# Layer 0's third projection of two batches beside the first chain of squarings; the first score projection starts with products of h alone; other fillers at the entry

## The chip, the cores and the metric

The kernel runs on one core of one Trainium2 chip. The metric is device time in microseconds of one launch. All matrix work is in float32 on the matrix engine (PE), where one product of a 128x128 stationary block with 512 columns takes two passes. The other engines are the vector engine (DVE), the scalar engine (ACT), GpSimd (POOL) and SyncE (SP, which issues DMAs).

## The reference

Four layers are applied to x of shape (8, 512, 32, 32); a batch is a matrix of 512 channels by 1024 positions. Cut to what matters here:

```python
# layer 0: three 1x1 convolutions to 64 channels, two of them with batch norm over all batches
f_x = relu(batchnorm(conv1x1(x, Wf, bf))).reshape(b, 64, hw)
g_x = relu(batchnorm(conv1x1(x, Wg, bg))).reshape(b, 64, hw)
h_x = conv1x1(x, Wh, bh).reshape(b, 64, hw)
z = einsum('bcn,bcm->bnm', f_x, g_x)
sigma = svd(z)[:, 0]                       # the largest singular value
x = conv1x1(einsum('bnm,bcm->bcn', z / sigma, h_x), Wv, bv) + x
# layer 1: group norm, attention over 1024 positions with 512 channels, projection, + x
# layer 2: attention with 128 channels, projection, batch norm by given constants, + x
# layer 3: signs of x times signs of W, batch norm, + x, a shifted leaky relu
```

## The kernel before

**Layer 0 without its big matrix.** z is never formed. With F, G and H the 64 x 1024 matrices of a batch, F Fᵀ, G Gᵀ and H Gᵀ are 64 x 64 (function `gram`, L1445 to L1463). The largest singular value comes from repeated squarings of the small matrix (F Fᵀ)(G Gᵀ). Two batches share the 128 partitions, so there are four pairs and four chains of squarings. `order` takes batches 6 and 7 first, then 0 to 5: the pair of batches 6 and 7 (named `jl`) has the chain `first_chain` (L1129 on), which must end before the first batch can go on. The other pairs (`rest`) have the chain `chain` (L1025 on); its steps are drawn one by one from the generator `behind`, wherever the main program calls `next(behind)` or `chore`.

**The loop over batches** (L1342 on). x of each batch is loaded and multiplied with the weights of f, g and h (L1354; 16 pieces for f and g, 8 for h, each writing half of the partitions). f and g are copied out and their statistics gathered (`bn_stats`). The product of h gets its bias on ACT as `hraw`, and in the next batch `turn` (L1248 to L1254) transposes it on PE in four blocks and copies it to `ht_pair`. x of the last two batches stays in SBUF (`resident`).

**Weights.** Layer 1's four weight matrices are merged into two: `wu` from q and k, `wo` from v and p. `natural` (L1320 to L1325) transposes q, k and v through two PSUM tiles of two banks each, every group of eight transposes copied out by ACT and DVE, half each. `product` (L1394 to L1407) makes a merged matrix in 16 products. After the loop the batch norm's mean, variance and scale are formed (L1490 to L1511), and `relu` (L1481) applies it on ACT to f and g of a batch.

**Fillers.** The chain of squarings is serial: two small products (L1141, L1142), copied out by DVE and ACT, which the next two need. So the generator `filler` holds PE work that is put between its steps: transposes of v, the products of `wu`, the Gram product of h and g of the pair `jl`, the scaling of a later weight, the transposes and Gram products of the other three pairs with the bias sums (`biases`) between, and the products of `wo`. This stretch is under a manual schedule for PE: the program's order is PE's order. DVE's and ACT's order is set by a scheduler when the program is built[...].

**Entry of the first batch** (`entering(0)`, `enter`). `weights0` (L299) makes two small weights from the chain's result, then four visits correct x: two products (L420), an addition on DVE (L429) and statistics (L432). Two small products with a group matrix (L441 mean, L448 variance) follow, then the scale and bias of the group norm. Between these steps PE gets a number of fillers given by the tuple `(2, 1, 1, 1, 2, 2, 4)`; what is left follows.

**First u.** `normal` (L471) forms the normalised h (not to be confused with layer 0's) in eight tiles on DVE; `split_h` makes the sums T1 to T4 (L336 to L339). `make_u` forms the score projection u in two groups of seven products each (Winograd's form of a 2 x 2 block product; `seven`, L342 to L380). Products named A11·B11 and A12·B21 read h alone, the other five need sums of h. In `make_u` for the first batch a step of the chains is drawn after its steps 1, 4, 7, 10 and 13; in the scores of the first batch after the steps 1, 5, 9, 17 and 24 (L923).

Of the kernel before, what the change touches and what calls it, by code (L numbers as in the profile page):

```python
# [8 lines left out]
F32 = mybir.dt.float32  # L9
F16 = mybir.dt.float16  # L10
I32 = mybir.dt.int32
AF = mybir.ActivationFunctionType
# [4 lines left out]
P = 128  # L17
B = 8
C = 512
N = 1024  # L20
CC = C // P
NT = N // P
HF = 512
NH = N // HF
# [61 lines left out]
def kernel(  # L86
# [17 lines left out]
    nc = tc.nc  # L104
    mm = nc.tensor.matmul
# [17 lines left out]
    def bank():  # L123
        return psum["bank"].tile([P, HF], F32, tag="bank", name="bank")
# [17 lines left out]
    def half(i):  # L142
        return bass.ts(i, HF)

    def side(i):

        return slice(i * MID, (i + 1) * MID)
# [11 lines left out]
    early = ctx.enter_context(ExitStack())  # L159
# [179 lines left out]
        tt(t4, b21, t2, ALU.subtract)  # L339
        return {"B11": b11, "B21": b21, "B22": b22, "T1": t1, "T2": t2, "T3": t3, "T4": t4}  # L340

    def seven(term, c11, c12, c21, c22, b1=None, b2=None, exp=None, then=None):  # L342

        def move(dst, ps, bias):
            if bias is None:
                nc.scalar.copy(dst, ps)  # L348
            else:
                nc.scalar.activation(dst, ps, AF.Identity, bias=bias)  # L350

        def plus(ps, bias, u, dst):
            if bias is None:
                nc.vector.tensor_tensor(dst, ps, u, ALU.add)  # L354
            else:
                nc.vector.scalar_tensor_tensor(dst, ps, bias, u, ALU.add, ALU.add)

        pa, va = term(None, "A11", "B11", True, False)
        move(c11, va, None)
        yield  # L360
        pc, vc = term(None, "S1", "T1", True, False)
        move(c22, vc, None)
        yield
        term(pa, "S2", "T2", False, False)
        move(c12, va, None)
        yield
        term(pc, "S4", "B22", False, True)
        plus(vc, b1, c12, c12)
        yield
        term(pa, "S3", "T3", False, False)  # L370
        plus(va, b2, c22, c22)
        yield
        _, vb = term(None, "A12", "B21", True, True)
        plus(vb, b1, c11, c11)
        yield
        term(pa, "A22", "T4", False, True)
        if exp is None:
            move(c21, va, b2)
        else:
            nc.scalar.activation(c21, va, AF.Exp, scale=exp)  # L380
        if then is not None:
            then()
        yield
# [94 lines left out]
        b = [ht[:, chunks[k], half(n)] for k in range(2) for n in range(2)]  # L478
        return differences_of(b, [hs[:, i] for i in range(3)])

    def make_u(env, hb, got):

        ut = env["big"].tile([P, CC, N], F32, tag="uv", name="ut")
        wa = weights["u"]

        def done():
            us = env["big"].tile([P, 3, 2, HF], F32, tag="us", name="us")
            got.append(
                sums_of(quarters_of(ut, chunks, [half(0), half(1)]), [us[:, i] for i in range(3)])
            )  # L490

        for i in range(2):
            term = product_of(
                lambda a, b, q, k: wa[a][:, k, bass.ts(i, P)],
                lambda a, b, q, k: hb[b][:, k, :],
            )
            yield from seven(
                term,
                ut[:, i, half(0)],
                ut[:, i, half(1)],  # L500
                ut[:, 2 + i, half(0)],
                ut[:, 2 + i, half(1)],
                bu[:, i : i + 1],
                bu[:, 2 + i : 3 + i],
                then=done if i else None,
            )

    def make_v(hb, vt):

# [383 lines left out]
    def fast(env, n, hb, ua):  # L893


        b = order[n]
# [4 lines left out]
        def chore(now):  # L901
            if now:
                next(behind, None)

        es = [None] * NT
        for k, _ in enumerate(scores1(env, hb, ua, es)):
            if rest3 and k % 2 == 0:
                if next(rest3[0], "end") == "end":
                    rest3.pop()
                    if more and order[n + 1] not in resident:  # L910
                        resident[order[n + 1]] = load_x(order[n + 1])
            if n == 0 and k == 2:
                weights["o"] = sums_of(quarters_of(wo, chunks, cols2), [so[:, i] for i in range(3)], True)
            if n == 0 and k == 6:
                tp = quarters_of(sbw["tpg"], chunks, [slice(0, P), slice(P, 2 * P)])
                weights["tp"] = sums_of(tp, [sp[:, i] for i in range(3)], True)
            if k == 8 and more:
                ahead = entering(n + 1)


            if k in (10, 13, 20, 27):
                next(ahead, None)
            chore(n == 0 and k in (1, 5, 9, 17, 24))  # L923
        esum = es.pop()
        vt = env["big"].tile([P, NT, C], F32, tag="uv", name="vt")
        for k, _ in enumerate(make_v(hb, vt)):
# [415 lines left out]
    for b in range(B):  # L1342
        xt = load_x(b) if b else first
        for name, src, pool in later.get(b, ()):
            load_w(name, src, shapes.get(name, [P, CC, C]), pool)
        if b == 4:
            load_rows()
        if b >= B - 2:
            resident[b] = xt
        banks = [bank() for _ in w0]  # L1350

        def products(i, cc):
            for h in range(NH):
                mm(  # L1354
                    out=banks[i][side(h), :],
                    lhsT=w0[i][:, cc, :],
                    rhs=xt[:, cc, half(h)],
                    start=cc == 0,
                    stop=cc == CC - 1,
                )  # L1360

        if b == 0:
            for cc in range(CC):
                for i in range(2):
                    products(i, cc)
        for i in range(3):
            if b == B - 1 and i == 2:
                for _ in natural("q", "w3"):
                    pass
            if b or i == 2:  # L1370
                for cc in range(CC):
                    products(i, cc)
            if i == 0:
                nc.scalar.copy(fs[b], banks[i])
                nc.vector.bn_stats(st[:, 0, b, :], fs[b])
            elif i == 1:
                nc.vector.tensor_copy(gs[b], banks[i])
                nc.vector.bn_stats(st[:, 1, b, :], gs[b])
                if last is not None:
                    turn(last[0], last[1], ht_pair[last[0] // 2], 0)  # L1380
        hraw = a2.tile([P, HF], F32, tag="hraw", name="hraw")
        nc.scalar.activation(hraw, banks[2], AF.Identity, bias=bhc)
        last = b, hraw
        if b == 3:
            total3 = sign_weights()
        if b == 5:
            scale_signs(total3)
# [102 lines left out]
        nc.vector.bn_aggr(mv[:, i, :], st[:, i, :, :])  # L1490
    nat_k = natural("k", "q")
    next(nat_k)
    turn(last[0], last[1], ht_pair[last[0] // 2], 0)
    ps = bank()
    mm(out=ps[:, 0:2], lhsT=fold, rhs=mv[:, :, 0], start=True, stop=True)
    nc.vector.tensor_copy(mean, ps[:, 0:2])
# [36 lines left out]

    cols2 = [slice(0, C // 2), slice(C // 2, C)]

    def filler():

        yield from natural("v", "k")  # L1540
        load_w("p", w_p, [P, CC, C], a1, tag="v")
        yield from product(nat["q"], nat["k"], wu, True)
        yield from gram(jl, 2, ht_pair[jl], gtl)
        scale_z()
        yield
        between = biases()
        sums = sums_u()
        for j in rest:
            for _ in grams(j):
                next(sums, None)  # L1550
                yield
                if next(between, None):
                    yield
        yield from product(nat["v"], sbw["p"], wo, False)
# [11 lines left out]
    with tc.manual_schedule(engines={mybir.EngineType.PE}):  # L1566
        steps = entering(0)
        for k, _ in enumerate(first_chain(jl)):

            for _ in range(4 if k == 3 * NSTEP + 3 else 2 if k % 3 == 1 or k == 0 else 1):  # L1570
                next(todo, None)
            for args in (next(relus, None),):
                if args:
                    relu(*args)
        for n in (2, 1, 1, 1, 2, 2, 4):
            next(steps)
            for _ in range(n):
                next(todo, None)
        for _ in todo:
            pass  # L1580
# [9 lines left out]
    with ExitStack() as main:  # L1590
        psum_pools(main, 0, 8)
        big = main.enter_context(tc.tile_pool(name="big", bufs=1, reuse_waits="tile"))
        epool = main.enter_context(tc.tile_pool(name="epool", bufs=EBUFS))
        small = main.enter_context(tc.tile_pool(name="small", bufs=3))
        env.update({"big": big, "e": epool, "small": small})
        got = []
        hb = split_h(env, normal(env, resident[order[0]], True))

        for k, _ in enumerate(make_u(env, hb, got)):
            if k in (1, 4, 7, 10, 13):  # L1600
                next(behind)
        ua = got[0]
        for n in range(B):
            hb, ua = fast(env, n, hb, ua)
# [171 lines left out]
```

## Time and profile before

| | us |
|---|---|
| median of 3 runs | 1883.69 |
| lowest to highest | 1883.57 to 1885.51 |
| profiled execution, time | 1883.24 |
| profiled execution, span first to last instruction | 1881.5 |

The profiled execution as time stretches (us from the span's start), with the lines of the code:

| stretch | what runs |
|---|---|
| 4.9 to 97.3 | loop over batches; q is transposed from 91.9 |
| 97.3 to 102.9 | last transposes of h, transposes of k and v, scale of the batch norm |
| 102.9 to 112.9 | first products of wu, relu on ACT, Gram products of the pair jl |
| 112.9 to 157.3 | first chain of squarings and its fillers |
| 157.3 to 182.7 | weights of the entry, corrections, group norm, products of wo |
| 182.7 to 210.9 | h and first u |
| 210.9 to 265.8 | scores of the first batch |

From there every batch takes the same steps. The granted PE clock is 1.00 from 8 us on, but for one stretch in the entry (a window of 170 to 180 us shows 0.83) and the end. In a line of the timeline the first figure is the start, the second the duration, then engine, line, operation, what is written from what, shape and count; a bracket gives the idle time before on that engine and who ended it. PE counts are passes.

### The profile page before, as it was taken

To read this page: it belongs to the slowest core of one execution; us is meant where nothing else is said; L and a number is where in the kernel's file an instruction comes from. 1 tells how busy PE (TensorE), PEld (TensorE's weight loads), DVE (VectorE), ACT (ScalarE), POOL (GpSimd) and SP (SyncE) were. 2 spreads that over 40 slices of the span, in tenths; PEclk is the share of its full clock that TensorE was granted. 3 is DMA by queue.
4 is the path that set the end of the run, shared out by engine and by line. 5 is a ranking of instruction groups with operands and counts; after the bars stand their busy time and mean duration, and the time that the engine had idled before them with its cause. 6 is when DMAs were issued, how large, how long until landed. Compare 5 with 4: busy or idle time off the path is not lost.

```text
span 1881.5 us, 16558 instructions
## 1 busy us (share of the span) xinstructions
PE 1857.0 (99%) x6244; PEld 952.1 (51%) x6244; DVE 1118.1 (59%) x2077; ACT 545.7 (29%) x888; POOL 121.8 (6%) x109
## 2 busy tenths in 40 slices
PE   8998999999999999999999999999999999999997
PEld 3365455544645455544645455544645464544653
DVE  3256776467764676567764676357643666355447
ACT  2142221144202521244202522144202521244113
POOL 1000001100020000100020001100020001000011
PEclk9999999999999999999999999999999999999999
DMA  8420000002000200002000200001000200000001
GB/s 324 161 79 7 1 18 1 1 34 73 12 1 12 84 23 1 1 34 73 12 1 11 78 30 0 1 34 67 12 0 12 90 12 0 1 34 23 12 0 47
DMA packets 25203, 66.51 MB, mean 35 GB/s; under 512 B 3553, under 2 KB 4765, under 8 KB 24477
## 3 DMA queue, kind: packets, MB, share of 16 engines
q1 hardware_dynamic: 24188, 64.96, 9.5%
q8 instruction: 51, 0.84, 0.2%
q10 hardware_dynamic: 864, 0.43, 0.1%
q14 instruction: 36, 0.29, 0.0%
q0 software_dynamic: 64, 0.00, 0.0%
HBM read 46.44 MB, written 18.94 MB: 35 GB/s over the span
## 4 chain that ended last, share of the span: by engine, by line
PE 96%; DVE 2%; ACT 1%; issue 0%; DMA 0%; POOL 0%; DVEq 0%; ACTq 0%
PE bank L396 46%; PE bank L565 21%; PE bank L967 6%; PE bank L814 6%; PE bank L1354 5%; PE bank L666 3%; PE bank L683 3%; PE bank L420 1%; PE bank L706 1%; PE wide L1394 1%; PE bank L1450 1%; PE bank L1035 1%; PE bank L837 0%; PE quad L1248 0%; PE bank L1141 0%
## 5 line engine op out<-in xcount | busy, mean ns | idle before, releaser
L565 PE MATMUL bank<-e,vt 128*128 128x512 f32 x768 | 336.2, 594 | 0.0
L565 PEld LDWEIGHTS bank<-e,vt 128*128 128x128 f32 x768 | 144.3, 190 | 172.3 <-issue 167.9
L396 PE MATMUL bank<-ut,h 128*128 128x512 f32 x384 | 178.3, 597 | 0.0
L396 PEld LDWEIGHTS bank<-ut,h 128*128 128x128 f32 x384 | 71.3, 190 | 95.2 <-issue 93.5
L814 PE MATMUL bank<-tpg 128*128 128x512 f32 x256 | 115.4, 595 | 0.0
L396 PE MATMUL bank<-us,hs 128*128 128x512 f32 x256 | 115.3, 592 | 0.0
L967 PE MATMUL bank<-e,tpg 128*128 128x512 f32 x256 | 114.7, 595 | 0.0
L354 DVE TENSOR_TENSOR e<-bank,e 128x512 f32<-128x512 f32 x96 | 66.1, 689 | 63.2 <-PE bank L396 44.7
L821 ACT ACTIVATE e<-bank 128x512 f32<-128x512 f32 x128 | 76.3, 597 | 67.0 <-PE bank L814 67.0
L396 PE MATMUL bank<-wo,h 128*128 128x256 f32 x384 | 89.9, 384 | 0.0
L348 ACT COPY e<-bank 128x512 f32<-128x512 f32 x96 | 56.1, 584 | 115.0 <-PE bank L396 114.6
L396 PE MATMUL bank<-h,wu 128*128 128x512 f32 x192 | 89.4, 595 | 0.0
L236 POOL TENSOR_TENSOR r_r<-r_v,minus_half 128x4 f32<-128x4 f32 (+1 forms) x11 | 10.9, 988 | 1073.4 <-DVE r_v L235 1067.9
L967 PEld LDWEIGHTS bank<-e,tpg 128*128 128x128 f32 x256 | 48.1, 190 | 60.4 <-issue 60.0
L396 PEld LDWEIGHTS bank<-us,hs 128*128 128x128 f32 x256 | 48.6, 190 | 58.4 <-issue 55.7
L396 PEld LDWEIGHTS bank<-wo,h 128*128 128x128 f32 x384 | 71.4, 190 | 12.6 <-issue 3.8
L826 DVE TENSOR_TENSOR esum<-esum,e 128x1024 f32<-128x1024 f32 x48 | 58.8, 1225 | 30.2 <-ACT e L821 30.0
L814 PEld LDWEIGHTS bank<-tpg 128*128 128x128 f32 x256 | 47.6, 190 | 55.0 <-issue 52.4
L694 ACT ACTIVATE sg<-xt,rb 128x512 f16<-128x512 f32 x64 | 44.2, 716 | 107.4 <-DVE xt L685 104.5
L354 DVE TENSOR_TENSOR vt<-bank,vt 128x512 f32<-128x512 f32 x48 | 33.2, 691 | 67.3 <-PE bank L396 66.6
L348 ACT COPY vt<-bank 128x512 f32<-128x512 f32 x64 | 37.3, 583 | 122.3 <-PE bank L396 122.3
L348 ACT COPY ut<-bank 128x512 f32<-128x512 f32 x48 | 28.1, 585 | 123.4 <-PE bank L396 123.4
(367 smaller groups left out, 2927.0 us busy)
## 6 DMA issues: line engine op xcount, KB each, us to landing
xt<-in_x SPq DMA_DIRECT2D x55, 512.0 KB
out<-both SPq DMA_DIRECT2D x63, 256.0 KB
rfull<-r_dram SPq DMA_DIRECT2D x15, 512.0 KB
f_dram<-f SPq DMA_DIRECT2D x8, 256.0 KB
fb<-f_dram SPq DMA_DIRECT2D x8, 256.0 KB
w<-in_w SPq DMA_DIRECT2D x1, 1024.0 KB
q<-in_w_q SPq DMA_DIRECT2D x1, 1024.0 KB
k<-in_w_k SPq DMA_DIRECT2D x1, 1024.0 KB
```

Of the source, the lines that this page charges most:

```text
L348: nc.scalar.copy(dst, ps)
L354: nc.vector.tensor_tensor(dst, ps, u, ALU.add)
L396: mm(out=ps[:, q * w : (q + 1) * w], lhsT=lt(ka, kb, q, k), rhs=rhs(ka, kb, q, k), start=first and q == 0 and k == 0, stop=last and k == 1 ...
L565: mm(out=ps, lhsT=a[:, t, bass.ts(r_, P)], rhs=e[t], start=first and t == 0, stop=last and t == NTH - 1, skip_group_check=True,)
L666: mm(out=ps[:, i, :], lhsT=xt[:, cc, bass.ts(4 * h + i, P)], rhs=sbw["tpg"][:, cc, 2 * P : 3 * P], start=cc == 0, stop=cc == CC - 1,)
L683: mm(out=ps, lhsT=sbw["z"][:, bass.ts(oc, P)], rhs=att, start=True, stop=True)
L694: nc.scalar.activation(sg[:, cc, :], xt[:, cc, half(h)], AF.Sign, bias=rb3[:, cc : cc + 1])
L814: mm(out=ps, lhsT=pt[:, 0, bass.ts(t, P)], rhs=tt[:, 0, half(h)], start=True, stop=True,)
L821: nc.scalar.activation(e[:, half(h)], ps, AF.Exp, scale=float(P) ** -0.5)
L826: nc.vector.tensor_tensor(esum, esum, e, ALU.add)
L967: mm(out=banks[h], lhsT=gt[:, t, :], rhs=es[t][:, half(h)], start=t == 0, stop=t == NT - 1,)
L1354: mm(out=banks[i][side(h), :], lhsT=w0[i][:, cc, :], rhs=xt[:, cc, half(h)], start=cc == 0, stop=cc == CC - 1,)
```

## The change

The products of h for batches 6 and 7 leave the loop; a generator `late_h` makes them as fillers, one quarter at a time, between the products of `wu` and the Gram product that needs them. The loop takes two banks instead of three for these batches, and the transposes of `hraw` for batches 5, 6 and 7 move accordingly (that of batch 5 stays in the loop, those of 6 and 7 go into `late_h`). `seven` can draw its sixth step (A12·B21) ahead to second place, and `make_u` with `early` takes the first two steps of both groups first, then the rest of each. The first u draws no chain steps any more; the scores of the first batch draw ten instead of five. The entry's tuple of fillers gets larger.

```diff
-    def seven(term, c11, c12, c21, c22, b1=None, b2=None, exp=None, then=None):
+    def seven(
+        term, c11, c12, c21, c22, b1=None, b2=None, exp=None, then=None, early=False
+    ):
...
+        def second():
+            _, vb = term(None, "A12", "B21", True, True)
+            plus(vb, b1, c11, c11)
+
         pa, va = term(None, "A11", "B11", True, False)
         move(c11, va, None)
         yield
+        if early:
+            second()
+            yield
...
-        _, vb = term(None, "A12", "B21", True, True)
-        plus(vb, b1, c11, c11)
-        yield
+        if not early:
+            second()
+            yield
...
-        for i in range(2):
+        def group(i):
...
+        groups = [group(i) for i in range(2)]
+        for _ in range(2 * early):
+            for g in groups:
+                next(g)
+                yield
+        for g in groups:
+            yield from g
...
-            chore(n == 0 and k in (1, 5, 9, 17, 24))
+            chore(n == 0 and k in (1, 4, 7, 9, 11, 15, 17, 19, 23, 25))
...
-        banks = [bank() for _ in w0]
+        banks = [bank() for _ in w0[: 3 if b < B - 2 else 2]]
...
-            if b == B - 1 and i == 2:
-                for _ in natural("q", "w3"):
-                    pass
+            if i == 2 and b >= B - 2:
+                if b == B - 1:
+                    for _ in natural("q", "w3"):
+                        pass
+                continue
...
-    turn(last[0], last[1], ht_pair[last[0] // 2], 0)
...
+    def late_h(b):
+
+        ps = bank()
+        for cc in range(CC):
+            for h in range(NH):
+                mm(
+                    out=ps[side(h), :],
+                    lhsT=w0[2][:, cc, :],
+                    rhs=resident[b][:, cc, half(h)],
+                    start=cc == 0,
+                    stop=cc == CC - 1,
+                )
+            if cc < CC - 1:
+                yield
+        hraw = a2.tile([P, HF], F32, tag="hraw", name="hraw")
+        nc.scalar.activation(hraw, ps, AF.Identity, bias=bhc)
+        yield
+        turn(b, hraw, ht_pair[b // 2], 0)
...
         yield from product(nat["q"], nat["k"], wu, True)
+        for b in order[:2]:
+            yield from late_h(b)
         yield from gram(jl, 2, ht_pair[jl], gtl)
...
-        for n in (2, 1, 1, 1, 2, 2, 4):
+        for n in (2, 2, 2, 2, 4, 3, 6):
...
-        for k, _ in enumerate(make_u(env, hb, got)):
-            if k in (1, 4, 7, 10, 13):
-                next(behind)
+        for _ in make_u(env, hb, got, True):
+            pass
```

More of the change, by code (lines that the diff above doesn't have):

```diff
@@ L479, in split_h, with make_u @@
         return differences_of(b, [hs[:, i] for i in range(3)])
-    def make_u(env, hb, got):
+    def make_u(env, hb, got, early=False):
         ut = env["big"].tile([P, CC, N], F32, tag="uv", name="ut")
@@ L496, in make_u @@
             )
-            yield from seven(
+            return seven(
                 term,
@@ L505, in make_u @@
                 then=done if i else None,
+                early=early,
             )
+        groups = [group(i) for i in range(2)]
[5 more added lines that the diff above has]
+            yield from g
     def make_v(hb, vt):
@@ L1380 @@
                     turn(last[0], last[1], ht_pair[last[0] // 2], 0)
-        hraw = a2.tile([P, HF], F32, tag="hraw", name="hraw")
-        nc.scalar.activation(hraw, banks[2], AF.Identity, bias=bhc)
-        last = b, hraw
+        if b < B - 2:
+            hraw = a2.tile([P, HF], F32, tag="hraw", name="hraw")
+            nc.scalar.activation(hraw, banks[2], AF.Identity, bias=bhc)
+            last = b, hraw
+        else:
+            last = None
         if b == 3:
@@ L1534 @@
     cols2 = [slice(0, C // 2), slice(C // 2, C)]
+    def late_h(b):
[11 more added lines that the diff above has]
+                yield
+        hraw = a2.tile([P, HF], F32, tag="hraw", name="hraw")
+        nc.scalar.activation(hraw, ps, AF.Identity, bias=bhc)
+        yield
+        turn(b, hraw, ht_pair[b // 2], 0)
     def filler():
```

## The prediction

> **What bounds the kernel now.** I read the page first (engine shares, the chain that ended last), then the waits of PE, then windows and the timeline of the first 300 us. The chain is PE almost throughout, and PE is busy in 99% of the span, so an edit that moves no work off PE can gain only where PE stands still:
>
> ```profile
> PE 1857.0 (99%) x6244; PEld 952.1 (51%) x6244; DVE 1118.1 (59%) x2077; ACT 545.7 (29%) x888; POOL 121.8 (6%) x109
> PE 96%; DVE 2%; ACT 1%; issue 0%; DMA 0%; POOL 0%; DVEq 0%; ACTq 0%
> ```
>
> The waits of PE in the first 320 us (who waited for whom: total, times, longest) name two long ones, both in the stage that the change touches:
>
> ```profile
> PE bank L441 <- DVE mv L440: 2.8, 1, 2.8
> PE bank L396 <- DVE hs L336: 2.3, 1, 2.3
> PE bank L1141 <- ACT gg_full L1460: 1.0, 1, 1.0
> ```
>
> The timeline shows both (start, duration, engine, line; in brackets the idle time before and what ended it). At 175.28 the group means wait for DVE's last statistics; the four passes behind them take 3.39 us instead of about 1.7. At 187.00 the second product of the first u waits for T1, which DVE forms after all of h:
>
> ```profile
> 175.28 0.59 PE L441 MATMUL bank<-mv,gmat 128*128 128x4 f32 x2 [2.85 <-DVE mv L440]
> 175.73 3.39 PE L1394 MATMUL wide<-p,nat_v 128*128 128x512 f32 x4
> 187.00 1.98 PE L396 MATMUL bank<-hs,su 128*128 128x512 f32 x4 [2.28 <-DVE hs L336]
> ```
>
> Windows around them give the price of the first (the figure after the POOL column is the granted clock):
>
> ```profile
> 172.30:175.28 2.98, 0.13 (x2) 0.00 (x1) 2.85 (x7) 0.00 (x0) 0.00 (x0) 0.99 0.14 52
> 175.28:178.60 3.32, 3.32 (x6) 1.77 (x7) 0.69 (x5) 0.00 (x0) 0.00 (x0) 0.50 0.00 0
> 184.50:187.00 2.50, 0.22 (x1) 0.00 (x0) 2.47 (x5) 0.58 (x1) 0.00 (x0) 1.00 0.00 0
> ```
>
> So the entry loses 2.98 us of standing, then 3.32 us at half clock (1.66 us lost), then 2.45 us (last pass starts at 184.13, takes 0.43): **7.1 us**. Smaller stalls stand in the first chain, and one in the scores:
>
> ```profile
> 130.81 0.66 PE L1248 MATMUL quad<-ident,f 128*128 128x128 f32 x4 [0.31 <-DVE z L1309]
> 134.14 1.15 PE L1450 MATMUL bank<-ft 128*64 128x64 f32 x32 [0.67 <-ACT gt L1252]
> 215.97 0.43 PE L1035 MATMUL bank<-cur,gm 128*128 128x64 f32 x2 [0.53 <-DVE gm L1047]
> ```
>
> [...] Here 97.30 to 102.86 holds almost only transposes, at clock 1.00; longer stretches this trace does not show.
>
> **The change part by part**, walked along the instruction order of the built program with durations of the trace.
>
> *(a) Entry.* The last pair's 16 transposes and three Gram products leave the first chain and follow the first chain's scaled matrix; the 16 products of wo all come after. Between the first correction product (L420 before) and the group means PE now has 4 x 1.06 us of corrections, three Grams of 1.08, seven products of 0.86 and switching of about 0.4: 13.9 us. DVE needs 11.0 us there (164.20 to 175.22), plus five or so evictions, some 1.4: 12.4. PE arrives about 0.8 us after DVE has finished. The wait and the slow clock go: +2.98 +1.66. After it come three products (2.6 us) over a DVE step of 1.2, and six (5.2 us) over the 4.0 us from 178.96 to the second tile of h at 183.0. Both are covered.
>
> *(b) First u.* It starts with A11·B11 and A12·B21 of both groups: four steps of 1.72 us, 6.9 us that need h alone. T1 is ready 2.8 us after the start (six more h tiles at 0.47, the 1.22 us sum, less the 1.1 us that PE comes late). +2.45, and nothing late next: T2 to T4 follow every 1.1 us, PE asks every 1.7.
>
> *(c) h of two batches leaves the loop.* Removed before the first weight product (102.86): h products of 3.5 and 3.6 us and two groups of transposes of 0.55, 8.2 us. But the last h products covered evictions. With them gone, q, k and v are turned in one run, each group of eight transposes waiting for a DVE copy (0.69) two groups back, DVE having the mean, variance and scale between them. Walked through: g ends at 87.9, q's first DVE copy ends at 90.3, k's at 92.9, v's at 95.0 to 95.7. The product starts near 95.7: 7.2 earlier, not 8.2. Then ACT: the scaled relu passes (0.8 each) are ready before the chain, three of them instead of one ahead of the copy that starts the chain, and one copy of nat_v behind four. The chain starts near 106.3 instead of 112.94: 6.6 for 8.2. **-1.5**. x of the last batch is no limit: its loads end by 80, its products now start at 80.9.
>
> *(d) h in the chain.* Eight pieces of 2 matmuls as fillers. A piece costs 0.47 + 0.52 us by the first and last pair of the run at 93.73, against 0.89 in one run: 8 x 0.1 = **-0.85**. Worse is the tail of each batch: eviction, transposes, and for the second the Gram that reads them stand directly one behind another on PE. The trace has these steps apart:
>
> ```profile
> 97.49 0.69 ACT L1382 ACTIVATE hraw<-bank,bhc 128x512 f32<-128x512 f32 x1 [3.07 <-PE bank L1354]
> 98.24 0.65 PE L1248 MATMUL quad<-ident,hraw 128*128 128x128 f32 x4
> 98.93 0.69 DVE L1254 COPY ht<-quad 128x512 f32<-128x512 f32 x1 [3.79 <-PE quad L1248]
> ```
>
> From the products' end (97.3) to the transposes: 0.95, in which PE before turned k; from the transposes' end (98.67) to the copy's: 0.95. In the new order nothing stands between: 2 x 0.95 + 1.0 = **-2.9**. Bounds: 0 if one of the chain's own steps slid in, which program order excludes, so -2.5 to -3.3.
>
> *(e) The rest of the chain.* The sums of wu now run during the h pieces and no longer hold z: of the stalls of pair one (0.47, 0.40, 0.84 start to start) the first two go: +0.8. The stall of the last pair (0.4) goes as its transposes leave: +0.5 with its neighbour. The table load before Ln now comes behind a Gram eviction, 1.1 us later; the fillers (3.8 us) just miss it: -0.25.
>
> *(f) Chain steps moved into the scores.* Five steps of the second chain leave u; batch 0's scores hold ten instead of five. PE cost is the same. DVE gets 5 x 1.6 = 8 us more in a stretch where it is busy 42.0 of 53 us, and steps stand 3.44 us apart. PE product, ACT copy, DVE transposes need 2.3 us, so DVE may be 1.3 us late each time. Walked through: margins of 0.6, 1.6, 0 and, at the last pair behind the statistics and two sums, -0.85. The 0.70 at 215 goes. **-0.2**; bounds +0.7 and -7.
>
> *Sum:* +7.1 +0.8 +0.5 -0.25 -1.5 -0.85 -2.9 -0.2 = 2.7 us. The profiled execution took 1883.24 (span 1881.5), so it becomes about 1880.6; on the median 1883.69 that is **1881.0**, 0.14% less. What a measurement of this kernel can tell from no change is about 0.2%, 3.8 us: the forecast lies inside it.
>
> **Rivals.** *R1, the costs are half* (0.3): the natural run and the relu queue cost nothing much and the scores none; then 7.1 + 1.3 - 3.7 + 0.5, about 5 us: 1878.5. For it: the costs of (c) are walks through queues, the gains are measured waits. Against: (d) alone takes 3.7 surely. *R2, DVE is late in the scores, slower* (0.1): if in (f) the statistics of batch 1 stay ahead of the chain's transposes, each of seven close steps stops PE 1.3 us or more over its margin; 9 us lost against 2.9 gained: 1888 to 1890. It decides from the point where DVE is later than 1.3 us after ACT's copy. Against: four of the gaps are wide, and 215.97 waited only 0.53. *R3, the gap stays* (0.12): the DVE statistics, now started among evictions, end after PE's 13.9 us; 1 to 2 us of wait return, or the clock falls in the 7.8 us of turning q, k and v (half clock for 3.4 us, at most 1.7): gain 1, 1882.7, no change.
>
> **How the numbers follow.** Forecast 0.48, R1 0.3, R3 0.12, R2 0.1. The forecast's own spread is 2 us, and a quarter of it falls below 1879.9; R1 lies there mostly. Faster 0.4, same 0.49, slower 0.11. Range 1877.3 to 1885.0: from all of R1 but its end to the forecast's far side.
>
> **What would show it.** Right: no wait for mv and none for hs, clock 1.00 through the entry; two waits of about 1 us for hraw and one for ht near 122 and 129; the first product of wu near 95.7 and the chain near 106.3. Wrong: a slow-clock window while q, k, v are turned (R3); waits for gm of over 1 us in the scores (R2); the chain's start before 105 (R1).

## The result and the profile after

The changed kernel takes 1878.8 us (median of 11 executions, 1878.24 to 1880.7), the kernel before in the same session 1883.89 (11 executions): ratio 0.9974, interval 0.9965 to 0.9983. That is 5.1 us or 0.26% less, just over the 0.2% that the prediction gives as what a measurement of this kernel can tell. The forecast of 1881.0 was 2.2 us too high; its range held the time. The profiled execution took 1878.7 us with a span of 1876.8 (before 1883.24 and 1881.5).

The page first, the shares of the engines and the chain of the work that ended last:

```profile
PE 1856.3 (99%) x6244; PEld 952.5 (51%) x6244; DVE 1118.4 (60%) x2077; ACT 545.4 (29%) x888; POOL 121.9 (6%) x109
PE 96%; DVE 2%; ACT 1%; DMA 0%; issue 0%; POOL 0%; DVEq 0%; ACTq 0%
```

PE has the same 6244 passes, 0.7 us less busy time and a span shorter by 4.7 us: no work went away, PE stands still less. What it waits for in the first 320 us behind the first load (total, times, longest; the waits of 0.2 us left out) is a different list from the one before:

```profile
PE quad L1266 <- ACT hraw L1573: 1.6, 2, 0.8
PE quad L1266 <- DVE ft L1272: 0.6, 1, 0.6
PE bank L1053 <- DVE gm L1065: 0.6, 1, 0.6
PE bank L1473 <- DVE ht L1272: 0.5, 1, 0.5
PE wide L1417 <- DVE nat_v L1343: 0.4, 1, 0.4
PE bank L1473 <- DVE gt L1272: 0.3, 1, 0.3
PE bank L1159 <- ACT gg_full L1483: 0.3, 1, 0.3
```

The 2.8 us for `mv` and the 2.3 for `hs` are gone, the 1.0 for `gg_full` is 0.3. New are the two waits for `hraw` and the one for `ht`. The timeline of PE shows where they stand:

```profile
95.61 2.84 PE L1417 MATMUL wide<-nat_k,nat_q 128*128 128x512 f32 x6 [0.37 <-DVE nat_v L1343]
...
104.97 0.49 PE L1159 MATMUL bank<-gg_full,gm 128*128 128x128 f32 x2 [0.25 <-ACT gg_full L1483]
...
125.79 0.66 PE L1266 MATMUL quad<-ident,hraw 128*128 128x128 f32 x4 [0.79 <-ACT hraw L1573]
...
133.31 0.66 PE L1266 MATMUL quad<-ident,hraw 128*128 128x128 f32 x4 [0.79 <-ACT hraw L1573]
...
134.75 1.15 PE L1473 MATMUL bank<-gt,ht 128*64 128x64 f32 x30 [0.52 <-DVE ht L1272]
...
172.20 0.30 PE L450 MATMUL bank<-mv,gmat 128*128 128x4 f32 x2
...
180.39 7.03 PE L405 MATMUL bank<-h,wu 128*128 128x512 f32 x16
187.26 3.60 PE L405 MATMUL bank<-hs,su 128*128 128x512 f32 x8
```

In the kernel before, the first product of wu and the first chain stand here:

```profile
102.86 2.84 PE L1394 MATMUL wide<-nat_k,nat_q 128*128 128x512 f32 x6
...
112.94 0.38 PE L1141 MATMUL bank<-gg_full,gm 128*128 128x128 f32 x1 [1.02 <-ACT gg_full L1460]
```

So the first starts 7.25 us earlier, the second 7.97. The group means at 172.20 and the second part of u at 187.26 start without a wait. Two windows of the changed kernel (length, then busy time and count of PE, PEld, DVE, ACT and POOL, the granted clock, DMA) give the clock where q, k and v are turned, and from the chain's end to u:

```profile
87.90:95.61 7.71, 6.80 (x55) 5.65 (x53) 6.70 (x22) 3.50 (x6) 0.70 (x1) 1.00 0.00 0
155.14:180.39 25.25, 25.25 (x169) 12.85 (x169) 18.79 (x48) 2.98 (x5) 1.02 (x1) 1.00 0.04 12
```

In the entry PE is busy without a break and at clock 1.00; before, a window there had 0.50.

A ledger shows which stretch gave what. Between two marks it adds, over all passes of PE, the time from one start to the next less an ideal time of the pass: 0.43 us for 128x512 (the 16 at 180.39 take 6.87 us start to start), others by their columns, and a half or a quarter of that where the block has only 64 or 32 rows or columns in use. The ideals are an estimate; rows of the changed kernel, start to start at clock 1.00, lie near them or above: 64 passes of 128x128 (at 1815.37) take 7.15 us, 0.112 each against 0.107; 32 of `128*64` with 512 columns (80.87) 7.02 us, 0.219 against 0.215; eight of `64*128` with 512 columns (230.12) 1.91 us, 0.239 against 0.215; eight of `128*32` with 256 columns (268.25) 0.57 us, 0.071 against 0.054. What passes take beyond the ideals (two of 4 columns 0.16 us at 172.20) is in both figures alike, so only the differences count. Two stretches are taken together where the change moves fillers from one to the other.

| stretch | before | after | gain | predicted |
|---|---|---|---|---|
| 80 us to the start of the first chain | 4.68 | 4.51 | +0.2 | -1.5, part (c) |
| first chain to the first product of u | 18.71 | 16.58 | +2.1 | +1.9, parts (a) +4.64, (d) -3.75, (e) +1.05 |
| first u and scores, to the values | 7.99 | 5.31 | +2.7 | +2.25, parts (b) and (f) |

The sum, 5.0 us, is there at the first product of the values, where the batch's attention is formed from the scores (292.28 before, 287.23 after).

### The profile page after: what moved, and what is told of

It is laid out like the page before. It is cut to its first block, busy times and chain, and to the rows that moved or that the text cites. A ratio compares the mean times of both kernels' runs of the same rounds, so it can differ in the third digit from the quotient of the medians.

```text
span 1876.8 us, 16564 instructions
## 1 busy us (share of the span) xinstructions
PE 1856.3 (99%) x6244; PEld 952.5 (51%) x6244; DVE 1118.4 (60%) x2077; ACT 545.4 (29%) x888; POOL 121.9 (6%) x109
## 4 chain that ended last, share of the span: by engine, by line
PE 96%; DVE 2%; ACT 1%; DMA 0%; issue 0%; POOL 0%; DVEq 0%; ACTq 0%
PE bank L405 46%; PE bank L583 21%; PE bank L832 6%; PE bank L985 5%; PE bank L1372 4%; PE bank L684 3%; PE bank L701 3%; PE bank L429 2%; PE bank L724 1%; PE wide L1417 1%; PE bank L1053 1%; PE bank L1473 1%; PE bank L855 0%; PE quad L1266 0%; PE bank L1563 0%; PE bank L1159 0%
```

## The experiments

Four theories were set against each other. **A**: the gain is the cover of the entry and of u (7.1 us), paid for in part by the waits and switches that h brings into the chain. **B**: the gain is that the chain starts earlier. **C**: moving h only costs, and the other two edits alone would do better. **D**: the chain's own latency sets its length, so that taking the new waits out uncovers nothing. All kernels are the changed one with one edit undone or added, or with two or three of these together. Positions are compared from the first product of wu on, since its own start varies by up to 1.25 us between the profiles of kernels that are alike up to there. Not the first load makes this: the first pass starts at 4.66 us in the changed kernel and at 4.58 in the one with the chain's steps back in u, but its first 32 passes take 8.6 us and 9.9. A median of few executions can move by as much.

**The first u in its old order.**

```diff
-        for _ in make_u(env, hb, got, True):
+        for _ in make_u(env, hb, got):
```

> The changed kernel, with the first u in its old order (A12B21 sixth in each group, one group after the other). Theory A (the gain is the entry's cover): since nine fillers now stand before u, PE comes later to h, and T1, ready at 183.0 in the changed kernel's trace, is late only by 183.0 less (180.4 + 1.7), so about +1.0 us, 1879.8, with one wait for hs of 0.8 to 1.0; not the 2.3 of the kernel before. Rival B (the early products alone carry the 2.3 us wait): +2.4 us, 1881.2.

Measured: 1880.25 us (1879.12 to 1882.1), ratio to before 0.9983, 0.9976 to 0.999: 1.45 us more than the changed kernel. The waits of PE name the stall:

```profile
PE bank L405 <- DVE hs L336: 0.8, 1, 0.8
```

Start to start it is 0.95 us, and the whole way to the values is 1.07 us longer. So the early products of u are worth about 1 us here, not the 2.45 that the kernel before lost at this place. T1 is ready 8.0 us after the product of the variance in both kernels, but with the larger tuple PE comes to u 5.4 us after it instead of 3.8.

**The old tuple of fillers at the entry.**

```diff
-        for n in (2, 2, 2, 2, 4, 3, 6):
+        for n in (2, 1, 1, 1, 2, 2, 4):
```

> The changed kernel with the old numbers of fillers (2, 1, 1, 1, 2, 2, 4). Theory A: between the first correction and the group mean PE has 4 x 1.06 + 3 x 1.08 + 1.72 + 0.5 = 9.7 us against DVE's 12.4: the wait for mv returns with 2.5 to 2.8 us, and with it a slow clock window (1.6 us lost): +4.2 us, 1883.0, clock 0.5 for 3.4 us. Rival B (the gain comes from the chain starting 8 us earlier, the entry is incidental): no change, 1878.8.

Measured: 1882.62 us (1881.67 to 1885.65), ratio 0.9996, 0.9988 to 1.0005: most of the gain is lost, against B, since the chain starts as early as in the changed kernel (9.36 us behind the first product of wu). The wait for the group's statistics is back, but no half clock follows it in this profiled execution:

```profile
171.18 0.39 PE L450 MATMUL bank<-mv,gmat 128*128 128x4 f32 x2 [1.97 <-DVE mv L449]
171.42 1.96 PE L1417 MATMUL wide<-p,nat_v 128*128 128x512 f32 x4
```

Four passes behind it take 1.96 us; in the kernel before they took 3.39. From the first product of wu to the values it is 2.80 us longer than in the changed kernel, without the half clock that A had counted in its 4.2.

**h of the last two batches back in the loop**, the new tuple and the new u kept.

```diff
-        for b in order[:2]:
-            yield from late_h(b)
...
-        banks = [bank() for _ in w0[: 3 if b < B - 2 else 2]]
+        banks = [bank() for _ in w0]
```

> The changed kernel with the products of h of the last two batches left in the loop, as before; early u, the fillers' numbers and the chain steps as changed. Theory A: 16 products of wo alone must cover the entry; the larger numbers use them up before the variance, so the wait for mv (2.9) and its slow clock go, but a wait of about 4 us for h opens after the variance, perhaps with a slow clock of its own: 1881.2 to 1882.9. Rival B (the gain is the early start of the chain): as the kernel before, 1883.9, with the chain starting near 113. Rival C (moving h is only a cost, 4 us of tails and switching): 1875.

Measured: 1881.81 us (1880.78 to 1884.17), ratio 0.9994, 0.9985 to 1.0002. The chain starts at 113.03, as before. PE has work up to the means, but none is left after the variance:

```profile
177.80 0.39 PE L457 MATMUL bank<-dev,gmat 128*128 128x4 f32 x2
181.70 8.80 PE L405 MATMUL bank<-h,wu 128*128 128x512 f32 x16 [3.52 <-DVE h L480]
```

Half clock follows here as well (windows of the same kernel, from the end of the variance on):

```profile
181.70:182.60 0.90, 0.90 (x2) 0.46 (x3) 0.90 (x3) 0.00 (x0) 0.00 (x0) 1.00 0.00 0
...
183.50:185.00 1.50, 1.50 (x3) 0.64 (x2) 1.50 (x4) 0.44 (x1) 0.00 (x0) 0.50 0.00 0
```

C falls: the change loses 3.0 us without h in the chain. What h does there is to stand in for fillers that the entry then still has. A holds. This time alone does not speak against B, as its interval reaches the kernel before; the run with the old tuple does.

**The waits that h brings, taken apart.** The steps of `late_h` are drawn so that a chain step, the second batch's h or another pair's transposes stand between h's last product, the transposes of `hraw` and the Gram product that reads `ht`.

```diff
-        for b in order[:2]:
-            yield from late_h(b)
-        yield from gram(jl, 2, ht_pair[jl], gtl)
+        one, two = (late_h(b) for b in order[:2])
+        for g in (one, one, one, one, two):
+            next(g)
+            yield
+        next(one, None)
+        for _ in range(3):
+            next(two)
+            yield
         scale_z()
         yield
+        next(two, None)
...
-            for _ in grams(j):
+            for i, _ in enumerate(grams(j)):
                 next(sums, None)
                 yield
+                if j == rest[0] and i == 0:
+                    yield from gram(jl, 2, ht_pair[jl], gtl)
```

> The changed kernel with the tails of h set apart: between the last product of h and the transposes of hraw one step of the chain or the scaling of z, between the transposes and the Gram product that reads them the transposes of the next pair. Theory A: the two waits for hraw (0.8 each, 0.95 start to start) and the one for ht (0.5 to 0.7) go: -2.4 us, 1876.4. Rival D (the chain's own latency is the limit there, and its steps would wait instead): no change, 1878.8, with waits for both in their place.

Measured: 1876.26 us (1875.83 to 1878.15), ratio 0.9965, 0.9952 to 0.9979: 2.5 us less than the changed kernel by the medians, 2.70 by the profile up to the values. No wait for `hraw` and none for `ht` is left:

```profile
126.12 0.49 PE L1159 MATMUL bank<-both 128*128 128x128 f32 x2 [0.19 <-ACT both L1174]
126.44 0.39 PE L1160 MATMUL bank<-both 128*128 128x128 f32 x2
126.67 0.60 PE L1266 MATMUL quad<-ident,hraw 128*128 128x128 f32 x4
```

D falls. The three waits cost what they last, 2 x 0.95 + 0.7 us start to start, and a bare reorder of the same work takes them off. All five executions lie below all eleven of the changed kernel.

**The chain's steps back in u.**

```diff
-            chore(n == 0 and k in (1, 4, 7, 9, 11, 15, 17, 19, 23, 25))
+            chore(n == 0 and k in (1, 5, 9, 17, 24))
...
-        for _ in make_u(env, hb, got, True):
-            pass
+        for k, _ in enumerate(make_u(env, hb, got, True)):
+            if k in (1, 4, 7, 10, 13):
+                next(behind)
```

> The five chain steps go back from the scores into the first u, all else as in the changed kernel. Theory A (moving them is worth nothing): the wait for gm of 0.58 us in the scores goes and one of about 0.5 to 0.7 us near the start of the scores comes back: within 0.5 us of the changed kernel, 1878.3 to 1879.3. Rival (ten steps make DVE late in the scores, as in the slower case of the prediction): 1 us or more less than the changed kernel, 1877.8 or below. Second rival (the steps in u hold up the sums of h): a wait for hs comes back in u, 1880 or above.

Measured: 1879.27 us (1878.35 to 1880.81), ratio 0.9978, 0.9969 to 0.9987. From the first product of wu to the values it takes 191.54 us against 191.62: u is 1.51 longer, the scores 1.61 shorter. The wait for `gm` of 0.58 us goes. In its place PE stands twice for less, some 0.2 and 0.3 us start to start, which is too short for the list of waits:

```profile
212.61 0.43 PE L1053 MATMUL bank<-cur,gm 128*128 128x64 f32 x2
...
218.09 0.33 PE L1053 MATMUL bank<-cur,gm 128*128 128x64 f32 x2
218.55 1.98 PE L405 MATMUL bank<-ut,hs 128*128 128x512 f32 x4
```

Moving the steps is worth nothing either way.

**Later steps in the scores, and a copy moved to DVE**, on top of the kernel with the waits taken apart.

```diff
-            chore(n == 0 and k in (1, 4, 7, 9, 11, 15, 17, 19, 23, 25))
+            chore(n == 0 and k in (1, 4, 7, 9, 11, 15, 18, 20, 23, 25))
...
-            nc.scalar.copy(g[side(1), side(1)], ps[side(1), 0:MID])
+            copy = nc.vector.tensor_copy if i else nc.scalar.copy
+            copy(g[side(1), side(1)], ps[side(1), 0:MID])
```

> The kernel with the tails apart (1876.26), with two more edits: the seventh and eighth step in the scores stand one place later, and the copy of the second half of gg_full that starts the first chain is DVE's instead of ACT's. If the wait for gm comes from the statistics in front of DVE's transposes, one place (1.7 us) later removes it: -0.55; the copy gives -0.25 at the start of the chain: 1875.5. If PE only meets the next wait: 1876.3.

Measured: 1876.17 us (1875.77 to 1878.52), ratio 0.996, 0.9946 to 0.9974: no better than without the two edits. PE met the next wait for `gm`, and a longer one:

```profile
254.46 0.43 PE L1053 MATMUL bank<-cur,gm 128*128 128x64 f32 x2 [1.22 <-DVE gm L1065]
```

From the first product of u to the values this takes 0.87 us more than with the waits taken apart alone, which is more than the 0.42 us by which the copy lets the chain start sooner behind the first product of wu. The profiled execution (1878.52 us, the longest of the five) also lost some 1.7 us at half clock, as the last section shows.

**h in two pieces of four matmuls instead of four of two**, on the changed kernel.

```diff
-            if cc < CC - 1:
+            if cc == 1:
                 yield
```

> h of the last two batches in two pieces of four matmuls each instead of four pieces of two, all else as in the changed kernel. Each change between a chain product and a piece is priced at 0.1 us in the prediction and at about 0.19 in the trace of the changed kernel (a piece of two takes 1.0 us and the chain product after it 0.1 more, against 0.89 in one run). Four changes fewer: pieces and chain products of these two batches take 0.4 us less (prediction) or 0.75 less (trace). The fillers are four fewer, so that transposes and Gram products of the last pair come into the first chain and the entry gets products of wo in their place, shorter by some 0.2 us each: up to 0.6 us of the wait for mv at the mean may come back. Total 1878.1 to 1879.0; what decides is the time from the first piece to the Gram of gt and ht.

Measured: 1881.37 us (1880.74 to 1882.21), ratio 0.9989, 0.9982 to 0.9995: 2.6 us more, a miss. A merge of two pieces does save (a piece of two takes 1.01 us start to start, one of four 1.87: 0.15 for each of four merges), and a chain step now stands in one of the two `hraw` waits (0.95). But four fillers fewer mean that the chain, which takes one filler at every step whatever its length, uses up transposes, Grams and products that the entry then lacks. Waits of PE in this kernel:

```profile
PE bank L405 <- DVE h L480: 1.7, 1, 1.7
PE bank L1187 <- DVE diag L1183: 1.0, 1, 1.0
```

The expectation put the loss at the means; it fell behind the variance (1.7 us) and at the chain's end (1.0), and half clock followed the second, in windows of this kernel:

```profile
155.00:156.00 1.00, 0.97 (x9) 1.00 (x10) 0.31 (x3) 0.21 (x1) 0.00 (x0) 1.00 0.00 0
...
157.00:158.00 1.00, 1.00 (x11) 0.67 (x11) 0.48 (x1) 1.00 (x1) 0.00 (x0) 0.50 0.00 0
158.00:159.00 1.00, 1.00 (x26) 1.00 (x24) 0.45 (x2) 0.91 (x3) 0.00 (x0) 0.50 0.00 0
```

At half clock from about 156.6 to 160.0 PE loses 1.7 us. The sum, 1.7 + 1.0 + 1.7 - 0.6 - 0.95 = 2.85, is the 2.86 us that the way from the first product of wu to the values is longer in the profile. How much of the median's 2.6 the clock makes is open. The mean granted clocks on record (0.997 in 19 of the 21 executions, against 0.998 or 0.999 in 10 of 11 of the changed kernel) suggest a half clock in most of them, but do not place it.

**The copy alone on DVE**, on the changed kernel.

```diff
-            nc.scalar.copy(g[side(1), side(1)], ps[side(1), 0:MID])
+            copy = nc.vector.tensor_copy if i else nc.scalar.copy
+            copy(g[side(1), side(1)], ps[side(1), 0:MID])
```

> In the changed kernel the second half of gg_full is copied by DVE instead of by ACT behind the relu passes. The prediction let three relu passes of 0.8 us stand before this copy and charged most of 1.5 us to it and to the run of transposes. If the relu queue still costs that, the first chain starts 1 us earlier or more and the kernel takes 1878 or less. If the trace is right, that ACT is only 0.25 us late, the chain starts 0.25 earlier and the kernel takes 1878.6, no difference that can be measured.

Measured: 1877.94 us (1877.52 to 1878.78), ratio 0.9971, 0.9959 to 0.9982; 0.72 less by the profile up to the values. The chain starts without a wait:

```profile
104.57 0.38 PE L1159 MATMUL bank<-gg_full,gm 128*128 128x128 f32 x2
104.79 0.39 PE L1160 MATMUL bank<-gm,gg_full 128*128 128x128 f32 x2
```

The start is 0.42 us nearer to the first product of wu, and the wait of 0.2 us for `diag` is gone too. So the copy on ACT still cost the changed kernel 0.4 us at the chain's start, between the expectation's two cases (0.25 and 1 us). The time of 1877.94 lies in the case that expected 1878 or less, but 0.9 us between two medians cannot tell the cases apart; the start can.

**Both gains together**: the waits taken apart, the copy on DVE, the scores as in the change.

```diff
-            nc.scalar.copy(g[side(1), side(1)], ps[side(1), 0:MID])
+            copy = nc.vector.tensor_copy if i else nc.scalar.copy
+            copy(g[side(1), side(1)], ps[side(1), 0:MID])
```

> The tails apart (1876.26) and the copy of gg_full's second half on DVE (0.86 us less than the changed kernel by the medians, 0.72 in the profile), with the steps in the scores where the change puts them. If the two gains are independent: 1875.4 to 1875.6, and from the first product of wu to the first product of the values 188.2 us. If the chain's earlier start is only spent waiting at the transposes of pair one and two (0.46 and 0.33 us in the kernel with the tails apart): 1876.2.

Measured: 1876.84 us over 5 executions (1875.15 to 1877.48), ratio 0.9964, 0.9951 to 0.9978. By the profile, first product of wu to values, it takes 188.40 us against 188.92 with the waits taken apart alone and 191.62 in the changed kernel. Its profiled execution, 1875.32 us, is the shortest profile of the study, but the median is 0.6 us above the 1876.26 of the waits taken apart alone, and medians of five with a spread of 2.3 us cannot rank the two. All five executions of either lie below all of the changed kernel and of the kernel before.

## Why the prediction was right in kind and off in size

**What came as predicted.** Part (a): the wait for `mv` and the half clock are gone, 4.64 us. The margin was thinner than the 0.8 us predicted: DVE's last operation (171.90, 0.16 long) ends 0.14 us before PE arrives. The prediction's own figures leave 0.3, not 0.8: PE's 13.9 us count from 163.04, DVE's 12.4 from 164.20. That the wait went altogether is in part luck.

```profile
171.66 0.21 DVE L443 BATCH_NORM_AGGREGATE mv<-st 128x2 f32<-128x12 f32 x1
171.90 0.16 DVE L449 TENSOR_TENSOR mv<-mv,bo 128x4 f32<-128x4 f32 x1
```

Part (b): no wait for `hs`, and T2 to T4 are never late. But the experiments show that the 2.45 us were not this edit's alone: with the other edits in place it is worth 1.07. Part (d), the tails: 0.95 for each `hraw` as predicted, 0.7 for `ht` instead of 1.0, so -2.6 for -2.9. The waits for `hraw` stand at 125 and 132.5, some 3 us later than the prediction placed them. At both PE stood 0.79 us, and nothing that comes later in the program slid in ahead of the transposes: the piece of h behind the first four starts at 126.37, the Gram product behind the second four at 133.90. Part (f): one wait leaves at the start of the scores, one of 0.58 us comes at 239.97 behind the statistics; undoing it changes nothing.

**The step that failed** is the second half of part (c), the price of ACT's queue. Its first half was right: the run of q, k and v puts the first product at 95.61 (predicted 95.7), 7.25 us earlier for 8.05 us of work that left. Its second half let ACT's queue of relu passes delay the copy of `gg_full`, and had the chain start at 106.3, that is 10.6 us after the product. It took 9.36; the kernel before took 10.08. ACT's timeline in the changed kernel:

```profile
95.04 1.52 ACT L1504 ACTIVATE f<-f,bi,r_r 128x512 f32<-128x512 f32 x2 [0.39 <-DVE bi L1533]
96.46 1.50 ACT L1504 ACTIVATE g<-g,bi,r_r 128x512 f32<-128x512 f32 x2
...
102.46 1.52 ACT L1504 ACTIVATE f<-f,bi,r_r 128x512 f32<-128x512 f32 x2
103.89 0.80 ACT L1504 ACTIVATE g<-g,bi,r_r 128x512 f32<-128x512 f32 x1
104.71 0.21 ACT L1483 COPY gg_full<-bank 64x64 f32<-64x64 f32 x1
```

Three passes do stand ahead of the copy, as predicted. But the prediction prices each pass at the 0.8 us of its row, while two take 1.52 and the third starts 1.43 after the first: one every 0.71. ACT runs almost without a gap from 95.04 to the copy, with eleven passes, so a walk at 0.8 puts the copy up to 1.0 us late, of the 1.25 us by which the stretch was missed. And the relu passes begin 9.86 us earlier than before, the product only 7.25: the scale is known 2.6 us sooner with respect to PE, which pays for the two passes more in the queue. In the kernel before:

```profile
104.90 1.52 ACT L1481 ACTIVATE f<-f,bi,r_r 128x512 f32<-128x512 f32 x2 [1.57 <-DVE bi L1511]
...
112.68 0.21 ACT L1460 COPY gg_full<-bank 64x64 f32<-64x64 f32 x1
```

The kernel before itself lost 1.02 us at this copy, and the prediction quoted that wait but let it grow, where it shrank to 0.25. So part (c) is -0.1 by the starts (8.05 us left, 7.97 gained; +0.2 in the ledger, whose ideal times leave the switches out) where -1.5 was predicted.

**Two terms that were off and nearly cancel.** Part (d), the pieces: predicted 0.1 us each, with nothing for the chain's products behind them. Four rows of the changed kernel show the price:

```profile
118.85 1.08 PE L1563 MATMUL bank<-xt,h 128*64 128x512 f32 x4
119.86 0.49 PE L1159 MATMUL bank<-both 128*128 128x128 f32 x2
120.19 0.39 PE L1160 MATMUL bank<-both 128*128 128x128 f32 x2
120.50 1.08 PE L1563 MATMUL bank<-xt,h 128*64 128x512 f32 x4
```

A piece takes 1.01 from start to start against 0.89 in one run, and the chain's two products behind it 0.64, against 0.45 behind a product of wu (107.46 to 107.90 in the same timeline). Added up over the rows from 118.85 to 133.31, the pieces cost 0.8 us and the six pairs of chain products among them 1.0: 1.8 us, not 0.85, so part (d) took 4.4 us and not 3.75. On the other side stands part (e): by difference, 2.1 - 4.64 + 4.4, it brought +1.9 us and not +1.05. The Grams of the last pair, which paid the same switch (135.82 to 136.37 is 0.55), left the chain, and the prediction counted only their waits; how much of the +1.9 us this makes was not measured. The late table load before Ln, priced at -0.25, brought no wait: ACT has it at 151.07 (1.28 us long), and `wv` follows at 155.14 without a wait.

So of the 2.3 us between the forecast's gain (2.7) and the ledger's (5.0), 1.7 is part (c), 0.4 is the stretch of u and the scores, and 0.2 the rest. The rival with the costs at half, 1878.5, is what came about, by (c) and not by (d), which cost more than forecast; its sign, a chain that starts before 105, came at 104.97. The rival in which the clock falls while q, k and v are turned is refuted: that window shows 1.00. The slower rival in the scores is too: no wait there exceeds 0.6 us.

## What to carry to other kernels

Fillers between the steps of a serial chain are drawn by count, so a piece cut in two is a filler gained for a later gap: joining pieces saved 0.15 us each and opened waits of 1.7 and 1.0 us elsewhere. When work is moved next to its own consumer, look at the eviction between them: three such waits held 2.6 us here and left when one step of other work was put in each. Walk a queue by the distance of the starts, not by the durations of the rows, and take off the waits that the old queue already had.

## What was not expected of the hardware

The 7.71 us of turning q, k and v, transposes and two small products, kept the clock at 1.00 (87.90 to 95.61). The window of the kernel before with work of the same kind (97.30 to 102.86) shows 1.00 too, so the rival in which the clock falls there was the author's guess, with no row behind it.

Half clock did not follow every standing. Waits of 2.85 us (the kernel before) and 3.52 us (h in the loop) were followed by it, in the latter 0.95 us after work had resumed; one of 1.97 us (the old tuple, in its profile) was not. Four of the eleven profiles have a stretch at half clock between the loop over batches and the values, and in each it lasts 3.41 us (in the kernel before from 175.20 on). In the 3.41 us ahead of the fall PE stood for 2.77 us in the kernel before and for 2.46 with h in the loop. But half clock also came where PE had stood little in as long a stretch (0.96 us) or not at all. One case is the kernel with h in two pieces, behind a wait of 1.0 us. The other is the kernel with later steps in the scores, whose windows ahead of the entry show:

```profile
149.00:152.00 3.00, 3.00 (x66) 2.85 (x60) 0.69 (x6) 2.70 (x4) 0.00 (x0) 1.00 0.00 0
...
153.00:154.00 1.00, 1.00 (x4) 0.00 (x0) 0.03 (x1) 0.00 (x0) 0.00 (x0) 0.50 0.06 16
154.00:155.00 1.00, 1.00 (x6) 0.79 (x5) 0.66 (x1) 0.59 (x1) 0.00 (x0) 0.50 0.00 0
```

Before both lie some 8 us of transposes, Gram products with 64 columns, short chain products and sums with one column. The execution shown took 1878.52 us, the other four of this kernel 1875.77 to 1876.29. Whether these small products have a part in it was not tried; the same stretch kept 1.00 in the profiles of the other seven experiments. In the kernel before, 2.98 us of standing do come ahead of the half clock, as the prediction says; what makes the clock fall is not shown.

Executions of one kernel seem to differ in this too. With the waits taken apart, three executions have a mean clock of 0.998 or 0.999 and take 1875.83 to 1876.26 us, and two have 0.997 and take 1878.1 and 1878.15. With h in the loop, seven have 0.997 (1880.78 to 1881.81) and six 0.996 (1883.14 to 1884.17). A stretch of 3.41 us at half clock loses 1.7 us and takes 0.001 off the mean, so one more of them would fit; only the profiled executions show where a stretch lies, so this is not shown.
